# Four graph layers on one core: layer 1's output computed feature by feature, sums in a matmul of their own, two nodes per partition, and a new table of times

## The chip, the core and the metric

The kernel runs on one core of a Trainium2 chip. A core has five engines that each take their own instructions in order: TensorE (PE) multiplies matrices, VectorE (DVE), ScalarE (ACT) and GpSimd (POOL) work element by element, and SyncE (SP) starts the DMA transfers. The engines wait for each other through semaphores. The metric is the device time of one execution in microseconds (us); lower is better.

## What is computed

There are 64 graphs of 256 nodes with 512 features each. Every graph goes through four layers, and each layer adds its result to `x`. All numbers are 32-bit floats. Cut to what matters here:

```python
h = relu(layernorm(x))                                  # at the head of every layer
# layer 0
q, k = split(h @ Wqk.T); v = h @ Wv.T
x += softmax_over_nodes(sum_m((q @ k.T) * adj) / 8) * v
# layer 1: 8 heads of 64 features
feats = h @ W                                           # per head
dense = leaky_relu(e_self[i] + e_neigh[j], 0.2) - 1e10 * (1 - adj)
x += relu(softmax_over_j(dense) @ feats + b)            # heads side by side
# layer 2: 8 heads of 64 features
Xp = h @ Wp + bp; attn = tanh(adj * ((Xp @ C.T) @ Xp.T))
x += relu(attn @ Xp)
# layer 3
q, k = split(h @ Wqk); v = h @ Wv
x += softmax_over_nodes(sum(q * (adj @ k))) * v
```

The graphs do not depend on each other.

## The kernel before

One graph is cut into 140 named steps. `graph(b)` defines them, and each step issues a few instructions. Up to five graphs are in work at once, each in another layer. The order in which the steps are issued is written by hand: `TIMES` gives each step of a graph a time, `PERIOD` is the distance from one graph to the next, `FIRST` and `LAST` hold own times for the graphs at both ends, and `WEIGHTS` those for loading the weights. `Plan.run` sorts all steps by these times and chains the instructions of each engine in this order. The times are thus only an order: at run time an instruction starts when the one before it on its engine has been issued and its semaphores are there. If one of them waits, all behind it on the same engine wait.

Tiles come from fixed pools (`keep`): 8 PSUM banks (`bank`), 5 `xt` (a graph's `x`), 2 `hn`, 3 `ht`, 4 `pair`, and so on. `take` hands out the one that has been free longest, `done` gives it back.

What the change touches:

- **Node layout.** `load` (L629 to L634) puts node c*128+p on partition p. `adj` is loaded the same way. A second copy of it is loaded in 32-wide pieces (`blocks`), and `at` (L639) transposes it on DVE in 32x32 blocks.
- **Transposed activations.** Each layer's `st` (statistics, DVE), `rs`, `pw` (a power on POOL, L668), `sh`, `hn` (normalise, ACT, L680) make the normalised rows. `sq` (L613) transposes them in 32x32 blocks on DVE, `sw` (L700) writes the result to DRAM, and `ht` (L618, four DMAs in `gathered`) reads it back with the features on the partitions. Layer 2 does the same with `xp` (`sqx`, `swx`, `xpt`).
- **Matmul rows.** `rows` (L607) multiplies a chunk of 128 nodes of `ht`, as the stationary operand, by a weight of 128 to 512 columns, summed over four blocks of features.
- **Layer 1.** `fa`, `fb` compute the features and, in 16 more columns, the two score terms of each head; `fae`, `fbe` copy them out. A tile of `feats` has 65 columns per head: 64 features and a column of ones, set once (L464). `sendp` (L824, two transposes on PE), `senda` (L829, ACT) and `er` (L835) turn the score terms into rows in DRAM, and `enes` (L839, L840) reads these back to all partitions. `max0` to `max3` (L852) find the largest term of each row on DVE, `mxv` completes it, `mxp` (L873), `mxa` (L878) and `mr` (L884) turn it into rows, and `mb` (L888) reads them back to all partitions. For each pair p of heads, `ea` (L897, ACT) adds and applies the leaky relu, `eg` (L904, POOL) adds the mask `negt`, `eb` (L910, DVE) subtracts the maximum, `ex` (L916, ACT) takes the exponential.
- **Layer 1's output.** `po` (L928) multiplies with the exponentials as the stationary operand (128 nodes i) and 65 columns of `feats` as the moving one; the 65th column yields the sum of the weights. `pn` (L941, L945, DVE) divides by it and clips at zero, `pa` (L953, POOL) adds to `xt`.
- **Masks.** `neg` (L644), `negt` (L648) and `am` (L1094) run on POOL.
- **Layer 2's output.** `py` (L1030) already computes the other way round: 64 features of `xp` are stationary, 256 nodes move, and two heads fill the two halves of the partitions. `ye` (ACT, L1039) copies out with a relu; `sqy` (L1064), `swy` (L700) and `yr` (L1076) transpose through DRAM; `yg` (POOL, L1083) and `yv` (DVE) add to `xt`.

The matmul at the centre of the change is this:

```python
nc.tensor.matmul(po[:, h % 4, :], e[:, s, j, i * P:(i + 1) * P], feats[:, j, h, :],
                 start=(j == 0), stop=(j == NC - 1))
```

Of the kernel before, what the change touches and what calls it, by code (L numbers as in the profile page):

```python
# [9 lines left out]
F32 = mybir.dt.float32  # L10
# [13 lines left out]
UE = U + 1  # L24
# [12 lines left out]
PERIOD = 60.2  # L37
TIMES = {
    "load": 0.000, "at": 1.247, "st0": 5.280, "rs0": 5.300, "negt": 7.670, "pw0": 13.367, "sh0": 13.387,
    "hn0": 13.407, "sq0": 13.427, "sw0": 16.594, "ht0": 18.551, "qk1": 23.168, "qk0": 24.945, "qe0": 24.965,  # L40
    "qe1": 24.985, "pv01": 25.815, "score0": 27.291, "s0v": 27.311, "softp0": 29.436, "pv00": 31.771,
    "softv0": 32.366, "softa0": 33.344, "softw0": 35.861, "add0": 35.881, "st1": 39.861, "rs1": 39.881,
    "pw1": 40.011, "sh1": 40.031, "hn1": 40.638, "sq1": 43.586, "sw1": 46.132, "ht1": 57.350, "fa0": 57.370,
    "fa1": 57.371, "fb0": 57.372, "fae0": 57.934, "fae1": 58.840, "sendp": 58.860, "senda": 58.880, "er": 60.959,
    "neg": 61.845, "fb1": 64.147, "fbe0": 67.381, "enes": 67.749, "fbe1": 71.535, "max2": 74.244, "ea1": 75.256,
    "max0": 75.757, "max3": 76.069, "ea3": 77.200, "ea0": 78.017, "max1": 78.219, "mxv": 78.317, "mxp": 79.925,
    "ea2": 80.651, "eg2": 82.397, "mxa": 85.102, "eg0": 86.489, "mr": 87.558, "eg1": 88.075, "mb": 88.185,
    "eb0": 90.739, "eb2": 93.202, "ex0": 94.320, "eb1": 95.449, "eg3": 96.405, "po0": 97.573, "ex1": 97.708,
    "ex2": 99.827, "po2": 100.283, "eb3": 101.293, "ex3": 101.313, "po1": 102.298, "pn0": 106.351, "pa0": 108.061,
    "po3": 110.560, "pn1": 110.580, "pa1": 114.029, "st2": 114.049, "rs2": 114.069, "pw2": 114.089, "sh2": 117.872,  # L50
    "hn2": 117.892, "sq2": 120.365, "sw2": 126.933, "ht2": 134.926, "xp0": 134.946, "xp1": 140.660, "xe0": 141.890,
    "xe1": 147.360, "sqx": 147.380, "swx": 148.833, "xpt": 152.315, "xc": 161.371, "xcv": 174.104, "xca": 174.124,
    "ps0": 174.125, "tv1": 174.144, "ta1": 174.164, "tv0": 174.656, "ta0": 177.182, "ps1": 177.255, "tv2": 177.275,
    "ta2": 178.752, "tv3": 180.071, "ta3": 180.091, "am": 180.092, "py0": 181.534, "py1": 184.516, "ye0": 188.391,
    "ye1": 188.411, "sqy": 190.648, "swy": 192.764, "yr": 197.444, "yv": 199.505, "yg": 201.580, "st3": 202.086,
    "rs3": 203.471, "pw3": 205.848, "sh3": 205.868, "hn3": 207.396, "sq3": 207.856, "agg0": 209.112,
    "sw3": 211.920, "ga0": 215.679, "agg1": 217.655, "ht3": 218.179, "ga1": 220.247, "z0": 234.444, "z1": 245.189,
    "zv0": 245.866, "pv30": 248.297, "pv31": 251.239, "zv1": 261.554, "softp3": 263.233, "softv3": 264.096,
    "softa3": 267.934, "softw3": 282.911, "add3": 285.241, "store": 294.897,
# [3 lines left out]
    "wn0": 292.900, "mt0": 293.000, "wqk": 293.100, "mv0": 294.200, "wa": 294.700, "mm0": 295.100, "wv0": 295.500,  # L63
    "w11": 295.600, "w10": 296.200, "sa1": 296.700, "sa0": 297.000, "wn1": 298.500, "w13": 298.600, "mt1": 299.000,
    "b1": 299.400, "mv1": 299.500, "mm1": 299.800, "w12": 300.000, "sa3": 300.100, "sa2": 300.500, "w21": 300.700,
    "mk": 301.500, "c2": 301.800, "wn2": 303.200, "w20": 304.200, "mt2": 304.500, "mv2": 304.800, "mm2": 305.200,
    "wn3": 305.800, "mt3": 308.600, "w22": 309.100, "mv3": 309.500, "mm3": 309.600, "mkp": 310.600, "ma": 310.800,
    "w23": 311.300, "mkv": 313.400, "b2": 314.200, "room": 318.700, "wv3": 321.500,
# [3 lines left out]
        "load": 292.800, "st0": 293.300, "rs0": 293.400, "pw0": 293.500, "sh0": 293.600, "hn0": 293.700,  # L72
        "sq0": 293.800, "at": 294.000, "negt": 294.400, "sw0": 294.600, "ht0": 294.800, "qk0": 295.200,
        "qe0": 295.300, "qk1": 295.800, "qe1": 295.900, "score0": 296.000, "pv01": 296.100, "s0v": 296.400,
        "softp0": 296.500, "pv00": 296.800, "softv0": 296.900, "softa0": 297.100, "softw0": 297.200,
        "add0": 297.300, "st1": 297.400, "rs1": 298.000, "pw1": 298.100, "sh1": 298.300, "hn1": 298.700,
        "sq1": 298.800, "sw1": 299.600, "ht1": 300.300, "fa0": 300.900, "fae0": 301.300, "fa1": 301.600,
        "fae1": 301.700, "sendp": 302.200, "fb0": 302.300, "senda": 302.400, "er": 302.500, "enes": 303.300,
        "fbe0": 303.400, "ea3": 304.600, "ea2": 305.300, "neg": 305.500, "max1": 305.600, "ea1": 305.700,
        "max3": 305.900, "max0": 306.000, "max2": 306.100, "ea0": 306.500, "mxv": 306.600, "eg1": 306.800,  # L80
        "mxp": 307.100, "eg2": 307.200, "mxa": 307.500, "fb1": 307.700, "mr": 307.800, "eg3": 308.100,
        "mb": 308.400, "fbe1": 308.900, "eg0": 309.200, "eb1": 309.700, "eb2": 309.900, "eb0": 310.100,
        "eb3": 310.200, "ex2": 310.300, "ex0": 310.400, "ex3": 310.500, "ex1": 311.000, "po0": 311.100,
        "po2": 311.800, "po3": 312.100, "pn1": 312.800, "pa1": 313.000, "po1": 313.200, "pn0": 313.700,
        "pa0": 313.900, "st2": 315.100, "rs2": 315.700, "pw2": 315.800, "sh2": 316.000, "hn2": 316.400,
        "sq2": 317.100, "sw2": 318.500, "ht2": 320.700, "xp0": 322.900, "xe0": 323.000, "xp1": 323.100,
        "xe1": 324.200, "sqx": 324.300, "swx": 325.300, "xpt": 325.400, "xc": 327.200, "xcv": 327.300,
        "xca": 327.800, "ps0": 328.100, "tv1": 328.500, "tv0": 328.700, "ps1": 328.800, "ta1": 329.100,
        "tv2": 329.700, "ta0": 329.800, "py0": 329.900, "tv3": 330.400, "ta2": 330.600, "ta3": 330.800,
        "py1": 331.100, "ye0": 331.300, "ye1": 332.000, "sqy": 332.100, "am": 332.200, "swy": 333.400,  # L90
        "yr": 333.900, "yg": 334.700, "yv": 334.800, "st3": 335.000, "rs3": 335.600, "pw3": 335.700,
        "sh3": 336.100, "hn3": 336.200, "agg0": 336.500, "agg1": 336.800, "sq3": 337.200, "sw3": 337.500,
        "ht3": 338.900, "ga0": 339.400, "ga1": 339.700, "z0": 340.400, "zv0": 340.500, "z1": 340.900,
        "pv30": 341.200, "zv1": 341.400, "softp3": 341.800, "softv3": 342.000, "softa3": 342.100, "pv31": 342.200,
        "softw3": 342.400, "add3": 343.000, "store": 344.300,
    },
    {
        "load": 233.000, "st0": 233.700, "rs0": 233.900, "pw0": 234.100, "at": 234.300, "sh0": 234.700,
        "hn0": 234.800, "sq0": 235.200, "sw0": 235.500, "negt": 236.100, "ht0": 236.400, "qk0": 237.300,
        "qe0": 237.400, "qk1": 237.500, "qe1": 237.600, "score0": 237.700, "pv00": 238.700, "s0v": 239.100,  # L100
        "pv01": 239.500, "softp0": 240.600, "neg": 240.800, "softv0": 240.900, "softa0": 241.000,
        "softw0": 241.700, "add0": 241.800, "st1": 241.900, "rs1": 242.400, "pw1": 242.500, "sh1": 242.600,
        "hn1": 243.600, "sq1": 243.800, "sw1": 243.900, "ht1": 244.700, "fa0": 246.000, "fa1": 246.700,
        "fae0": 246.800, "fae1": 247.100, "sendp": 247.700, "senda": 248.000, "er": 248.100, "fb0": 248.600,
        "enes": 248.800, "fbe0": 249.100, "max2": 251.200, "ea3": 251.300, "max0": 251.400, "max1": 251.500,
        "max3": 251.700, "mxv": 252.300, "mxp": 252.400, "ea1": 252.500, "fb1": 253.100, "eg1": 253.300,
        "mxa": 253.600, "ea0": 254.200, "mr": 254.300, "ea2": 254.400, "eg2": 255.300, "mb": 256.400,
        "eg3": 256.500, "fbe1": 256.600, "eg0": 257.000, "eb2": 257.500, "eb0": 258.200, "eb3": 258.800,
        "ex2": 259.100, "eb1": 259.300, "ex3": 259.400, "po2": 259.500, "po3": 259.600, "ex0": 259.700,
# [308 lines left out]
def tile_four_gnn_layers(ctx: ExitStack, tc: tile.TileContext, x, adj, nodemask,  # L418
                         wqk0, wv0, w1, b1, a_self, a_neigh, w2, b2, c2t, wqk3, wv3, out):

    nc = tc.nc
    B = x.shape[0]

# [7 lines left out]
    rows_d = ctx.enter_context(tc.tile_pool(name="rows_d", bufs=12, space=DRAM))  # L434
    banks = ctx.enter_context(tc.tile_pool(name="banks", bufs=1, space=PSUM))

    plan = Plan(tc)

    def keep(kind, count, shape, pool=None):

# [728 lines left out]
```

## Time and profile before

| | |
|---|---|
| Median of three runs | 3894.62 us (3894.17 to 3900.92) |
| The profiled execution | 3905.45 us, of which its span 3903.3 us |
| Share of the span in which an engine is busy | PE 98%, DVE 78%, ACT 44%, POOL 32% |
| Mean busy share of the 16 DMA engines | 74.7% for the queue of SP |
| Packets under 512 bytes | 1493936 of 1657607 |

The span runs from the first to the last instruction in the profile. "Busy" counts the time in which an engine has an instruction under way; matmuls overlap, and their ends are modelled. A matmul of 32-bit floats appears as two instructions: `po` has 32 matmuls per graph, and the profile counts 4096 of them in 64 graphs. A line of the instruction groups gives source line, engine, operation, output and input, number, then the busy time in us and the mean duration of one in ns.

### The profile page before, as it was taken

Reading aid. Unit: us, or ns where it says so; the run is one execution under the profiler, and the core shown is the slowest. Engines: PE = TensorE matmul, PEld = TensorE weight load, DVE = VectorE, ACT = ScalarE, POOL = GpSimd, SP = SyncE. Lnnn points to the kernel's source line nnn. Section 1 sums busy time; section 2 is a strip of 40 time slices with the busy share of each in tenths; the row PEclk is TensorE's granted clock in tenths of the full one; section 3 lists DMA queues with packets and bytes.
Section 4 is the critical chain, followed back from the end, with each engine's and each line's share of the span. In section 5 each row is a group of like instructions: output and inputs, shape, how many; then the busy total and the mean of one; then the engine's idle time right before and its main releaser. Section 6 shows DMA issues by size and latency. Waiting matters only on the chain.

```text
span 3903.3 us, 53632 instructions
## 1 busy us (share of the span) xinstructions
PE 3811.1 (98%) x17474; PEld 2375.3 (61%) x17474; DVE 3033.7 (78%) x7641; ACT 1704.9 (44%) x3333; POOL 1264.8 (32%) x1098
## 2 busy tenths in 40 slices
PE   7999999999999999999999999999999999999989
PEld 4756566566566666666666666666566665665564
DVE  6887778777877877877777788788788778777774
ACT  2444444444444444444444444444444444444342
POOL 1332323323323323323323333333233233233231
PEclk9999999999999999999999999999999999999989
DMA  8666777777777788777777877777778777777754
GB/s 211 174 189 172 179 194 174 196 193 179 194 189 184 194 185 189 192 185 181 190 186 186 196 182 187 191 181 191 191 176 200 187 181 192 187 179 193 172 145 107
DMA packets 1657607, 717.62 MB, mean 184 GB/s; under 512 B 1493936, under 2 KB 1549296, under 8 KB 1632752
## 3 DMA queue, kind: packets, MB, share of 16 engines
q1 hardware_dynamic: 1657328, 714.19, 74.7%
q8 instruction: 140, 2.29, 0.3%
q14 instruction: 139, 1.14, 0.1%
HBM read 477.56 MB, written 236.45 MB: 183 GB/s over the span
## 4 chain that ended last, share of the span: by engine, by line
PE 74%; DVE 7%; DMA 4%; SPq 2%; issue 1%; POOL 1%; ACT 1%; DVEq 0%; POOLq 0%; ACTq 0%
PE bank L607 44%; PE bank L928 10%; PE bank L1016 6%; PE bank L1030 5%; PE bank L1102 5%; PE bank L994 3%; DVE junk L852 2%; DVE sq L613 1%; DMA hn<-sq_d 1%; SPq L618 1%; DMA ht<-sq_d 1%; DVE shift L673 1%; PE bank L768 1%; PE bank L718 1%; DVE stats L657 1%
## 5 line engine op out<-in xcount | busy, mean ns | idle before, releaser
L607 PE MATMUL bank<-w_s,ht 128*128 128x256 f32 (+2 forms) x3072 | 963.4, 464 | 30.6 <-DMA ht<-sq_d 24.5
L607 PE MATMUL bank<-wv_s,ht 128*128 128x512 f32 x2048 | 914.4, 594 | 0.1
L607 PEld LDWEIGHTS bank<-w_s,ht 128*128 128x128 f32 x3072 | 572.9, 192 | 364.4 <-issue 215.6
L607 PEld LDWEIGHTS bank<-wv_s,ht 128*128 128x128 f32 x2048 | 380.8, 191 | 426.2 <-issue 410.8
L904 POOL TENSOR_TENSOR pair<-pair,negt 128x1024 f32<-128x1024 f32 x256 | 600.5, 2367 | 50.6 <-ACT pair L897 46.4
L680 ACT ACTIVATE hn<-xt,shift,rstd 128x512 f32<-128x512 f32 x512 | 388.7, 806 | 448.6 <-DVE shift L673 430.3
L928 PEld LDWEIGHTS bank<-feats,pair 128*128 128x128 f32 x4096 | 485.0, 194 | 47.9 <-issue 25.5
L897 ACT ACTIVATE pair<-all,ec 128x256 f32<-128x256 f32 x1024 | 417.2, 494 | 200.1 <-DMA all<-er_d 196.3
L928 PE MATMUL bank<-feats,pair 128*128 128x65 f32 x4096 | 480.8, 276 | 10.2 <-ACT pair L916 10.2
L1055 ACT ACTIVATE pair<-pair 128x512 f32<-128x512 f32 x512 | 294.8, 623 | 420.6 <-DVE pair L1048 420.2
L852 DVE CUSTOM_DVE_ANT_0 junk<-all,adj 128x256 f32<-128x256 f32 x1024 | 444.0, 434 | 35.2 <-DMA all<-er_d 2.1
L607 PE MATMUL bank<-m_s,ht 128*128 128x512 f32 x1024 | 465.9, 599 | 1.3 <-DVE pair L1048 0.8
L668 POOL TENSOR_TENSOR rstd<-rstd,power 128x2 f32<-128x2 f32 x256 | 180.6, 706 | 813.4 <-DVE rstd L664 804.9
L1048 DVE TENSOR_TENSOR pair<-bank,at 128x512 f32<-128x512 f32 x512 | 327.4, 683 | 107.7 <-PE bank L1016 107.0
L1083 POOL TENSOR_TENSOR xt<-xt,hn 128x512 f32<-128x512 f32 x64 | 111.5, 1742 | 924.6 <-DMA hn<-sq_d 657.9
L613 DVE STREAM_TRANSPOSE sq<-hn 128x512 f32<-128x512 f32 x512 | 337.7, 690 | 58.9 <-ACT hn L680 58.9
L657 DVE BATCH_NORM_STATS2 stats<-xt 128x6 f32<-128x512 f32 x512 | 327.2, 680 | 36.4 <-POOL xt L1083 28.6
L910 DVE TENSOR_TENSOR pair<-pair,all 128x1024 f32<-128x1024 f32 x256 | 325.9, 1292 | 9.9 <-DMA all<-m_d 7.5
L607 PEld LDWEIGHTS bank<-m_s,ht 128*128 128x128 f32 x1024 | 189.2, 190 | 213.5 <-issue 207.1
L953 POOL TENSOR_TENSOR xt<-xt,o 128x256 f32<-128x256 f32 x256 | 181.2, 729 | 386.6 <-DVE rs L941 225.1
L916 ACT ACTIVATE pair<-pair 128x1024 f32<-128x1024 f32 x256 | 262.2, 1047 | 45.1 <-DVE pair L910 39.6
L1016 PE MATMUL bank<-xc,xpt 64*128 64x256 f32 x2048 | 255.8, 389 | 1.8 <-ACT xc L1002 1.0
(77 smaller groups left out, 3866.9 us busy)
## 6 DMA issues: line engine op xcount, KB each, us to landing
sq_d<-sq SPq DMA_DIRECT2D x384, 512.0 KB
ht<-sq_d SPq DMA_DIRECT2D x1024, 128.0 KB
all<-er_d SPq DMA_DIRECT2D x128, 1024.0 KB
all<-m_d SPq DMA_DIRECT2D x64, 1024.0 KB
xt<-in_x_dram SPq DMA_DIRECT2D x64, 512.0 KB
xpt<-sq_d SPq DMA_DIRECT2D x256, 128.0 KB
hn<-sq_d SPq DMA_DIRECT2D x256, 128.0 KB
out_dram<-xt SPq DMA_DIRECT2D x64, 512.0 KB
```

Source lines behind the costliest of these rows:

```text
L607: nc.tensor.matmul(p, ht[:, k, c * P:(c + 1) * P], w[:, k], start=(k == 0), stop=(k == KC - 1))
L613: nc.vector.transpose(sq.rearrange("p (r k c i) -> p c k r i", r=4, k=KC, c=NC)[:, c], t[:, c])
L657: nc.vector.bn_stats(stats[:, c, :], g["xt"][:, c, :])
L680: nc.scalar.activation(hn[:, c, :], g["xt"][:, c, :], AF.Relu, bias=st["shift"][:, c:c + 1], scale=st["rstd"][:, c:c + 1])
L852: nc.vector.tensor_tensor_reduce(junk, g["en"][:, h, :], g["adj"][:, c, :], 1.0, -BIG, OP.add, OP.max, st["mx"][:, c, h:h + 1])
L897: nc.scalar.activation(e[:, s, j, :], g["es"][:, h, :], AF.Prelu, bias=st["ec"][:, j, H + h:H + h + 1], alpha=0.2)
L904: nc.gpsimd.tensor_tensor(e, e, g["negt"][:, None].to_broadcast([P, 2, NC, N]), OP.add)
L910: nc.vector.tensor_tensor(e, e, g["m"][:, 2 * p:2 * p + 2, None, :].to_broadcast([P, 2, NC, N]), OP.subtract)
L928: nc.tensor.matmul(po[:, h % 4, :], e[:, s, j, i * P:(i + 1) * P], feats[:, j, h, :], start=(j == 0), stop=(j == NC - 1))
L1016: nc.tensor.matmul(ps[s][:, m, :], g["xpt"][half, p, m * P:(m + 1) * P], g["xc"][half, p, :], start=True, stop=True)
L1048: nc.vector.tensor_tensor(th[:, s], g[f"ps{p}{s}"].rearrange("p (m n) -> p m n", m=NC), g["at"], OP.mult)
L1055: nc.scalar.activation(g[f"th{p}"][:, s], g[f"th{p}"][:, s], AF.Tanh)
```

## The change

1. Node 2p+c is on partition p (before: node c*128+p). `load` and `store` move two nodes per partition in one piece. `chunk(t, c)` picks every second column, and every matmul that took 128 neighbouring columns of `ht`, `at` or `xpt` takes these. The DVE transposes write or read with a step of two, and `gathered` and `blocks` now move pieces of 64 numbers (before: 32).
2. `po` has the features as the stationary operand (64 columns) and 256 nodes of the exponentials as the moving one, two heads in the two halves of the partitions. The column of ones is gone.
3. The sums are computed apart: `eh` adds the two halves of the exponentials on POOL, `su` multiplies them by a 32-column tile with one column of ones, once per head, into the four quarters of a bank. `se` (ACT), `sp` (two transposes on PE) and `sr` (DVE) bring the reciprocals to the nodes' partitions.
4. `oe` (ACT) copies the output with a relu; `sqo`, `swo`, `or` bring it back to the nodes' partitions through DRAM, and `oa0`, `oa1` (POOL) multiply by the reciprocals and add to `xt`. `back` serves layers 1 and 2. `pn` and `pa` are gone.
5. `sendp` and `senda` become `send`, `mxp` and `mxa` become `mxt`: each is a transpose in 32x32 blocks on DVE. `er` and `mr` write in four DMAs each.
6. `neg`, `negt` and `am` move from POOL to ACT.
7. `TIMES`, `WEIGHTS`, `FIRST` and `LAST` are new throughout, and `PERIOD` is 59.0 (before: 60.2). There are now 150 steps.

```diff
-PERIOD = 60.2
+PERIOD = 59.0
...
-    small = ctx.enter_context(tc.tile_pool(name="small", bufs=6))
+    small = ctx.enter_context(tc.tile_pool(name="small", bufs=5))
...
+    def chunk(t, c):
+        return t.rearrange("p (n c) -> p c n", c=NC)[:, c]
...
-    keep("feats", 2, [P, NC, H, UE])
+    keep("feats", 2, [P, NC, D])
...
-    keep("o", 1, [P, NC, 4 * U])
+    keep("mx", 1, [P, NC, S])
+    keep("half", 2, [P, 2, N])
...
+    ones = consts.tile([P, 2, S], F32)
+    nc.gpsimd.memset(ones, 0.0)
+    for q in range(2):
+        nc.gpsimd.memset(ones[:, q, q:q + 1], 1.0)
...
-            nc.tensor.matmul(p, ht[:, k, c * P:(c + 1) * P], w[:, k], start=(k == 0), stop=(k == KC - 1))
+            nc.tensor.matmul(p, chunk(ht[:, k], c), w[:, k], start=(k == 0), stop=(k == KC - 1))
...
-            nc.vector.transpose(sq.rearrange("p (r k c i) -> p c k r i", r=4, k=KC, c=NC)[:, c], t[:, c])
+            nc.vector.transpose(sq.rearrange("p (r k i c) -> p c k r i", r=4, k=KC, c=NC)[:, c], t[:, c])
...
-            nc.sync.dma_start(t.rearrange("p k (c b i) -> b p (k c) i", c=NC, b=4)[i],
-                              sq_d.rearrange("(b d) (r f i) -> b (d r) f i", b=4, r=4, i=S)[i])
+            nc.sync.dma_start(t.rearrange("p k (b e) -> b p k e", b=4)[i],
+                              sq_d.rearrange("(b d) (r k e) -> b (d r) k e", b=4, r=4, k=KC)[i])
...
-            nc.sync.dma_start(g.take("xt"), x[b].rearrange("(c p) d -> p c d", p=P))
+            nc.sync.dma_start(g.take("xt"), x[b].rearrange("(p c) d -> p c d", c=NC))
...
-            nc.gpsimd.tensor_scalar(g.take("negt", HP), g["at"], -1.0, -NEG_BIG, op0=OP.add, op1=OP.mult)
+            nc.scalar.activation(g.take("negt", HP), g["at"], AF.Identity, scale=-NEG_BIG, bias=far)
...
+        def back(name, cols):
+            @step(f"sq{name}")
+            def _():
+                nc.vector.transpose(g.take("sq").rearrange("p (b k c i) -> p k b c i", b=4, k=HP, c=NC),
+                                    g[cols].rearrange("p k (b i c) -> p k b c i", b=4, c=NC))
+                g.done(cols)
+            @step(f"sw{name}")
+            def _():
+                out_by_squares()
+            @step(f"{name}r")
+            def _():
+                y = g.take("hn", NC, name="y" if name == "y" else "yo")
+                y = y.rearrange("p c d -> p (c d)").rearrange("p (a f) -> p a f", a=4)
+                for q in range(4):
+                    nc.sync.dma_start(y[q * S:(q + 1) * S], st["sq_d"].rearrange("(a i) (q f) -> q i a f", a=4, q=4)[q])
...
-        @step("sendp")
-        def _():
-            pn = g.take("bank", name="pn")
-            for c in range(NC):
-                nc.tensor.transpose(pn[:E, c * P:(c + 1) * P], st["ec"][:, c, :], ident)
...
+        @step("send")
+        def _():
+            st["er"] = er = work.tile([P, N // 4], F32, name="er", bufs=1)
+            nc.vector.transpose(er.rearrange("p (i c) -> p c i", c=NC), st["ec"])
...
-            nc.sync.dma_start(st["er_d"], st["er"])
+            for i in range(4):
+                nc.sync.dma_start(st["er_d"][:, i * 2 * S:(i + 1) * 2 * S], st["er"][i * S:i * S + E])
...
+                for j in range(NC):
                     for s in range(2):
                         h = 2 * p + s
-                        for j in range(NC):
-                            nc.tensor.matmul(po[:, h % 4, :], e[:, s, j, i * P:(i + 1) * P], feats[:, j, h, :],
-                                             start=(j == 0), stop=(j == NC - 1))
+                        nc.tensor.matmul(po[s * U:(s + 1) * U, p % 2, :], feats[:, j, h * U:(h + 1) * U],
+                                         e[:, s, j, :], start=(j == 0), stop=(j == NC - 1))
...
+            @step(f"eh{p}")
+            def _():
+                e = g[f"e{p}"]
+                nc.gpsimd.tensor_tensor(g.take("half", name=f"h{p}"), e[:, :, 0, :], e[:, :, 1, :], OP.add)
+                g.done(f"e{p}")
...
+            @step(f"su{q}")
+            def _():
+                if not q:
+                    g.take("bank", name="su")
+                for r in range(2):
+                    for s in range(2):
+                        t = 2 * r + s
+                        nc.tensor.matmul(g["su"][t * S:(t + 1) * S, :N], ones[:, q], g[f"h{2 * q + r}"][:, s, :],
+                                         start=(q == 0), stop=(q == 1))
...
+            @step(f"oe{q}")
+            def _():
+                if not q:
+                    g.take("cols", name="oc")
+                nc.scalar.activation(g["oc"][:, 2 * q:2 * q + 2, :], g[f"po{q}"].rearrange("p (r n) -> p r n", r=2),
+                                     AF.Relu)
...
+        def divide(c):
+            @step(f"oa{c}")
+            def _():
+                y = g["yo"].rearrange("p c d -> p (c d)").rearrange("p (a k c i) -> p c k a i", a=4, k=HP, c=NC)[:, c]
+                rs = st["rs"][:, c].rearrange("p q t -> p (q t)").rearrange("p (k s) -> p s k", s=2)
+                for s in range(2):
+                    half = y[:, :, 2 * s:2 * s + 2]
+                    nc.gpsimd.tensor_tensor(half, half, rs[:, s, :, None, None].to_broadcast([P, HP, 2, S]), OP.mult)
+                xt = g["xt"][:, c, :].rearrange("p (k a i) -> p k a i", k=HP, a=4)
+                nc.gpsimd.tensor_tensor(xt, xt, y, OP.add)
+                g.done("yo")
...
-                nc.gpsimd.tensor_scalar(g["at"][:, m, :], g["at"][:, m, :], mask_c[:, m, b:b + 1], None, op0=OP.mult)
+                nc.scalar.activation(g["at"][:, m, :], g["at"][:, m, :], AF.Copy, scale=mask_c[:, m, b:b + 1])
```

The order in which `TIMES` puts PE's steps in the new plan, written within one period (the number is how many periods after its graph's loading the step runs): fb1 (2), xc (3), po0, po1 (2), ps0 (3), po2, su0, po3 (2), ps1 (3), su1 (2), fa1, fa0 (1), sp (2), z0, z1 (4), py0, py1 (3), softp3, pv31, pv30 (4), qk0, qk1 (0), fb0 (1), score0 (0), xp0 (2), softp0 (0), xp1 (2), pv00, pv01 (0), agg1, agg0 (3).

## The prediction

> **What bounds the kernel now.** I read the page's busy times first, then the chain that ended last, then that chain in order of time, and last PE's timeline.
>
> ```profile
> span 3903.3 us, 53632 instructions
> PE 3811.1 (98%) x17474; PEld 2375.3 (61%) x17474; DVE 3033.7 (78%) x7641; ACT 1704.9 (44%) x3333; POOL 1264.8 (32%) x1098
> PE 74%; DVE 7%; DMA 4%; SPq 2%; issue 1%; POOL 1%; ACT 1%; DVEq 0%; POOLq 0%; ACTq 0%
> ```
>
> PE is busy for 98% of the span. That alone does not show a PE at its limit, because the ends of matmuls are modelled; but 74% of the chain that ended last is PE too. The same chain, with start and length of each piece:
>
> ```profile
> 559.33 5.59 PE bank L607 x24
> 564.92 0.22 PE bank L824 x2
> 565.14 3.60 PE bank L1030 x32
> 568.74 15.66 PE bank L607 x40
> 584.40 0.22 PE bank L873 x2
> ...
> 588.05 0.22 PE bank L718 x2
> ...
> 601.47 3.52 PE bank L928 x32
> 604.99 1.78 PE bank L994 x8
> 606.77 3.52 PE bank L928 x32
> 610.29 1.93 PE bank L1016 x16
> ...
> 617.78 5.59 PE bank L607 x24
> ...
> 2566.15 5.59 PE bank L607 x24
> ```
>
> The block of 24 (fa0, fa1, fb0) comes once per graph. From 559.33 to 617.78 are 58.45 us, filled by PE pieces without a gap: this is PE's work for one graph. From 559.33 to 2566.15 lie 34 graphs, 59.02 us each, so stalls cost 0.57 us per graph. 64 x 59.02 = 3777; the other 126 us of the span are the ends. Only what shortens PE's 58.45 us, or adds a stall to it, counts.
>
> **What the Trainium skill says.** "TensorEngine Tiling (Array Packing)", Tiling Modes: a stationary operand of 64 columns leaves room for two tiles, one of 32 for four, working at once. The trace agrees for 64: L1030 moves 256 columns in 3.60/32 = 113 ns, a full-width L607 of 256 columns takes 1.83/8 = 229 ns. No row shows 32. "TensorE: Matmul & The Clock Gate", Measured speedup vs the span model, has 2.38 for three column tiles. "SBUF — State Buffer", Door 1, states lines of 16 bytes, full rate with two reads per line; a step of two floats keeps two. The trace shows no such weight load; DVE's transposes of `hn` read every fourth float and take 690 ns for 512, about one per cycle. "GPSIMD Engine Reference", 3.1: about 2.6 cycles per element with two inputs; L904 takes 2367 ns for 1024, which fits.
>
> **PE, part by part, per graph.**
> - `po`: out go two L928 pieces of 3.52 us, 7.04. In come 16 matmuls, 32 instructions, of L1030's form: 3.60.
> - Transposes: out go L824 and L873, 0.44. In come `sp`'s two, as L718: 0.22.
> - `su`: 8 matmuls, 16 instructions of 256 columns. At 229 ns alone 3.66; four at once 0.92; in pairs 1.81. I take 1.2, since the skill's three tiles gain 2.38, so four about 3.
> - `chunk` changes the step of the weight loads and not their number: zero, discussed below.
>
> Sum: -7.04 + 3.60 - 0.44 + 0.22 + 1.2 = -2.46. PE's work falls from 58.45 to 56.0 us.
>
> **The other engines** must fit 56 us. DVE now 3033.7/64 = 47.4: minus `pn` (108.7+45.0)/64 = 2.4, plus `sqo` as L1064 1.24, `sr` as two L941 0.35, two small transposes about 0.45 (estimate from 512 in 690 ns and a fixed part): 47.0. POOL 19.8: minus `pa`, `am`, `neg`, `negt` (181.2+118.1+40.0+40.4)/64 = 5.9; plus four `eh` of 512 elements, between L953 (729 ns for 256) and L904, 1.28 each, 5.1; plus `oa`, per c two products (0.73 to 0.96 each) and an addition as L1083 (1.74), 6.4 to 7.3 in all: about 26. ACT 26.6: plus `neg`, `negt` as L680 1.6, `am` as L897 1.0, `oe` 1.2, `se` 0.36, minus two copies 0.72: 30. None reaches 56. SP gains six row writes (0.34 each), `swo` 0.33, `or` 4 x 0.44: 4.1 us of some 35 used. The DMA engines get fewer packets: about 25,900 per graph now, of which `ht` and `xpt` are 5 x 512 KB / 128 B = 20,480; that number halves, `blocks` halves, the new round trip adds about 640: some 15,000. I book no gain.
>
> **The added wait.** Layer 1's output now leaves PE, goes through DRAM and POOL, and only then can layer 2 normalise. From po3's end to xp0 the parts are `oe1` 0.60 (L1039), `sqo` 1.24, write and read back, `oa` 6.9, statistics to the last `ht` issue, landing. The read back is taken from layer 2's present one:
>
> ```profile
> 2053.75 0.66 SPq L700 DMA_DIRECT2D sq_d<-sq  x1
> 2054.51 2.26 SPq L1076 DMA_DIRECT2D hn<-sq_d  x4
> ```
>
> ```profile
> 2060.47 0.69 DVE L1083 TENSOR_TENSOR xt<-xt,hn 128x512 f32<-128x512 f32 x1 [3.11 <-DMA hn<-sq_d]
> ```
>
> That is 2060.47 - 2053.75 = 6.72. Statistics starting at 2019.15 had their `ht` issued by 2030.86:
>
> ```profile
> 2019.15 1.28 DVE L657 BATCH_NORM_STATS2 stats<-xt 128x6 f32<-128x512 f32 x2
> ```
>
> ```profile
> 2027.42 3.44 SPq L618 DMA_DIRECT2D ht<-sq_d  x4
> ```
>
> 11.71; and `ht` issued by 2002.04 let PE start at 2004.50, 2.46. Together 0.60+1.24+6.72+6.9+11.71+2.46 = 29.6. In the new order PE has between po3 and xp0: ps1 1.93, su1 0.6, fa1 and fa0 3.76, sp 0.22, z 6.9, py 3.60, softp3 0.22, pv 6.88, qk 1.78, fb0 1.83, score0 0.84: 28.6. So xp0 waits about 1.0 us per graph. Behind oa on POOL stands pw2 of the same chain; behind ht2 on SP stands yr, so layer 2's output of another graph, and DVE's yv, slip with it. If POOL or DVE hold each other up (sh, 0.16 us, once took 2.29 beside eg), the chain grows; with half the packets it shrinks. Bounds: 0 to 3 us.
>
> Two smaller waits are new. su1 needs the last `eh`: two of these after ex3 take 2.6 us on POOL, while PE has po3 and ps1, 2.8; I book nothing, up to 0.7 if `eh` costs as much as L1083. On ACT, `negt` waits for `at` and `am` for the last `tv`; both are done by DVE well before in the new order, and ACT is idle for half of the period, so what stands behind them (`ea`, `qe`) is not held: nothing.
>
> The other long returns have room. From pv01 to fa1 the chain is the last addition (0.7), statistics to `ht` (11.7), landing 2.5: 14.9, against agg 3.5, fb1 1.83, xc 1.78, four po 3.6, ps 3.86, su 1.2: 15.8. The stall of 0.57 that exists now is partly this kind; I keep none beside the 1.0, as xp0's wait gives the rest time, and put the error in the range.
>
> **Sum.** 56.0 + 1.0 = 57.0 per graph; 64 x 57.0 + 126 = 3774 for the span, 3776 for the execution, against its own 3905.45. That is -3.3%; the median shown, 3894.62, is 0.28% below the profiled run, so about 3765.
>
> **Rivals.**
> 1. The return is longer, 31 to 32 us, for instance because `or` lands late behind other transfers or POOL's products cost more: xp0 waits 2.5 us, 58.5 per graph, 3870 for the span, 3860 as a median. For it: POOL already waited 657.9 us in all for such a landing (`xt` L1083 on `hn<-sq_d`). Against: the packets halve. From 31.6 us on (28.6 + 3.0, which is 59.0 per graph) the kernel is not faster.
> 2. Slower: strided weight loads cost more. Place: the matmuls whose load is as long as their stream, qk (16 instructions, 1.78/16 = 111 ns each), score0 (8), ps (32), 56 per graph. At double length 56 x 0.11 = 6.2 us: 57.0 + 6.2 = 63.2, 4171 for the span, about 4160. It decides from 2.0/56 = 36 ns more per load. Against: the lines of 16 bytes, and DVE's full rate at a wider step. For: PE reads nothing this way now.
> 3. The sums do not run side by side: su costs 3.66, 2.46 more, PE's work 58.5; with the longer filling at xp0 (from su1) the wait falls to nothing: about 58.6 per graph, 3870. If the wait stays, 59.5 and slower, 3930.
>
> That the table itself is the cost, its order making waits that I haven't found, would look like rival 1.
>
> **How the numbers follow.** Forecast 57.0 per graph: 0.58, own range 55.9 to 58.0, 3695 to 3830. Rival 1: 0.25, of which 0.04 same and 0.06 slower. Rival 2: 0.11, nearly all slower, 0.01 faster. Rival 3: 0.06, of which 0.02 slower. Faster (by over 0.2%, about what a measurement of this kernel can tell from no change): 0.58 + 0.15 + 0.01 + 0.04 = 0.78; same 0.04; slower 0.06 + 0.10 + 0.02 = 0.18. The range from 3670 to 3940 leaves out rival 2 and the worst of rivals 1 and 3.
>
> **What would show it.** In PE's timeline: L928's successor in pieces of 32 instructions in 3.6 us; su's 16 in about 1.2; loads of ht still near 190 ns and qk's 16 in 1.8. PE's idle time before xp0, released by DMA `ht`, about 1 us per graph. The block of fa comes every 57 us. Wrong it would be if PE's pieces of L607 grow (rival 2), if su's piece is 3.6 (rival 3), or if PE stands idle for 2 us or more per graph, before xp0 or elsewhere (rival 1).

## The result: no change, and the profile after

The changed kernel took 3894.13 us (median of four runs, 3892.97 to 3897.74); the kernel before, beside it, 3894.39 us. The ratio is 0.9999 with a 95% interval of 0.9982 to 1.0016. The forecast was 3765. All times are medians of the executions in the fast state; this matters only for the single graph in experiment 5, where it makes the difference 11.9 us in place of the 10.9 that an earlier expectation gives.

The page after answers to the one before with these lines (the engines' busy time, then the engines' shares of the chain that ended last):

```profile
span 3892.8 us, 52870 instructions
...
PE 3677.6 (94%) x16322; PEld 2126.0 (55%) x16322; DVE 3060.4 (79%) x7449; ACT 1872.2 (48%) x3653; POOL 1531.4 (39%) x1229
...
PE 46%; DVE 20%; DMA 17%; SPq 8%; issue 5%; POOL 3%; ACT 2%; DVEq 0%; ACTq 0%; POOLq 0%
```

PE does 133.5 us less (3811.1 before), 2.1 us per graph. But the span is only 10.5 us shorter, and PE's share of the chain falls from 74% to 46%: it now waits for others. Here is that chain for part of a graph in the middle, with start and length of each piece:

```profile
2029.04 1.72 DVE shift L706
...
2042.19 3.91 PE bank L639 x16
...
2057.17 6.89 PE bank L639 x16
2064.06 0.02 issue
2064.08 0.53 SPq L650
...
2066.00 2.81 DMA ht<-sq_d
2068.81 0.25 issue
2069.06 3.68 PE bank L639 x8
```

There are two ways into PE here for which the forecast booked nothing. The block of `fa` at 2042.19 hangs on layer 1's `ht`, and that on a `shift` (the step `sh`) which holds the chain for 1.7 us at 2029.04; half of all `shift` take 0.16 or less. And xp0 at 2069.06 hangs on an `ht` whose transfer starts when the matmuls ending at 2064.06 (layer 3's `pv`) give a buffer back. In this example its data had landed only 0.1 us before. In the stretch from 600 to 3600 us SyncE, with the data of an `ht` landed, still waited for such a buffer 55 times, 29.5 us in all and 1.1 at most:

```profile
SPq L650 <- PE bank L639: 29.5, 55, 1.1
```

PE's longest waits in the same stretch, by what ended them (total, times, longest), after and then before:

```profile
PE bank L639 <- DMA ht<-sq_d: 51.5, 65, 1.5
PE bank L966 <- ACT pair L954: 26.1, 46, 1.0
```

```profile
PE bank L607 <- DMA ht<-sq_d: 11.5, 12, 1.7
```

The two after are 78 of PE's 91 us of idle time in that stretch; before it was 21 us in all. Counted over 48 graphs in the middle, PE now idles 1.76 us per graph: 1.00 between the end of pv01 and `fa` (for `ex` before `po`, and for `ht` before `fa`) and 0.76 before xp0.

To split the time, I took the distance from one graph to the next on PE's timeline (`agg` of graph 9 to `agg` of graph 59, divided by 50), and what 64 such distances leave of the span, "the ends". The ratios are to executions of the kernel before that were taken beside each run:

| run | median us | ratio to the kernel before, 95% | us per graph | PE idle, 600 to 3600 us | ends us |
|---|---|---|---|---|---|
| before | 3894.39 | | 59.03 | 21 | 125 |
| after | 3894.13 | 0.9999 (0.9982 to 1.0016) | 58.12 | 91 | 173 |
| a_nolock | 3838.32 | 0.9851 (0.9834 to 0.9868) | 57.23 | 57 | 175 |
| a_ht4 | 3870.30 | 0.9929 (0.9914 to 0.9944) | 57.84 | 82 | 163 |
| a_ht4_nolock | 3817.74 | 0.9802 (0.9786 to 0.9818) | 56.82 | 49 | 178 |
| a_noprod | 3884.08 | 0.9969 (0.9953 to 0.9984) | 58.11 | 92 | 158 |
| a_all_noprod3 | 3792.86 | 0.9744 (0.9727 to 0.9761) | 56.48 | 35 | 172 |
| b_nolock | 3876.37 | 0.9947 (0.9932 to 0.9962) | 58.74 | 15 | 114 |
| b_ht4_nolock3 | 3880.01 | 0.9965 (0.9950 to 0.9979) | 58.81 | 17 | 115 |
| b_layout | 3896.76 | 1.0003 (0.9996 to 1.0009) | 59.03 | 4 | 117 |

The names are those of the experiments below; a_ are edits of the changed kernel, b_ of the kernel before. So the forecast's span of 3774 us was missed by 119: 64 x (58.12 - 57.0) = 72 us in the steady part and 173 - 126 = 47 us at the ends.

This division is rough. The last of the 50 distances already belongs to the end of the run (49.9 us after, 56.0 before). Without it the time per graph is 58.28 us after and 59.09 before, the ends are 163 and 121 us, and the miss divides into 82 and 37. The kernel before was also profiled in an execution 11 us above its median, which makes 0.17 us per graph. What is left of the gain is about 0.64 us per graph, not 0.91. Differences between the a_ rows change by 0.03 us at most.

### The profile page after: what moved, and what is told of

It reads as the page before. It is cut to its first block, busy times and chain, and to the rows that moved or that the text cites. A ratio compares the mean times of both kernels' runs of the same rounds, so it can differ in the third digit from the quotient of the medians.

```text
span 3892.8 us, 52870 instructions
## 1 busy us (share of the span) xinstructions
PE 3677.6 (94%) x16322; PEld 2126.0 (55%) x16322; DVE 3060.4 (79%) x7449; ACT 1872.2 (48%) x3653; POOL 1531.4 (39%) x1229
## 2 busy tenths in 40 slices
DMA packets 967435, 784.71 MB, mean 202 GB/s; under 512 B 788913, under 2 KB 859121, under 8 KB 942577
## 4 chain that ended last, share of the span: by engine, by line
PE 46%; DVE 20%; DMA 17%; SPq 8%; issue 5%; POOL 3%; ACT 2%; DVEq 0%; ACTq 0%; POOLq 0%
PE bank L639 34%; DVE sq L645 7%; DMA ht<-sq_d 6%; SPq L650 5%; DMA sq_d<-sq 5%; PE bank L1111 4%; PE bank L966 3%; DVE pair L948 2%; DVE junk L896 2%; DMA hn<-sq_d 2%; PE bank L1097 2%; DVE stats L690 2%; DMA blocks<-in_adj_dram 2%; DVE xt L775 2%; DVE shift L706 1%
## 5 line engine op out<-in xcount | busy, mean ns | idle before, releaser
L639 PEld LDWEIGHTS bank<-w_s,ht 128*128 128x128 f32 x3072 | 587.4, 198 | 381.3 <-issue 288.2
L942 POOL TENSOR_TENSOR pair<-pair,negt 128x1024 f32<-128x1024 f32 x256 | 604.5, 2374 | 117.2 <-ACT pair L935 117.2
L639 PEld LDWEIGHTS bank<-wv_s,ht 128*128 128x128 f32 x2048 | 397.3, 197 | 444.8 <-issue 442.8
L975 POOL TENSOR_TENSOR half<-pair 128x512 f32<-128x512 f32 x256 | 331.3, 1306 | 593.1 <-PE bank L989 328.0
L896 DVE CUSTOM_DVE_ANT_0 junk<-all,adj 128x256 f32<-128x256 f32 x1024 | 472.8, 462 | 31.4 <-issue 0.2
L639 PE MATMUL bank<-m_s,ht 128*128 128x512 f32 x1024 | 455.5, 597 | 8.2 <-DMA ht<-sq_d 6.8
L935 ACT ACTIVATE pair<-all,ec 128x256 f32<-128x256 f32 x1024 | 433.4, 497 | 9.8 <-DMA all<-er_d 9.8
L966 PE MATMUL bank<-pair,feats 128*64 128x256 f32 x2048 | 272.4, 401 | 62.2 <-ACT pair L954 62.0
L954 ACT ACTIVATE pair<-pair 128x1024 f32<-128x1024 f32 x256 | 264.0, 1050 | 118.4 <-DVE pair L948 111.2
L948 DVE TENSOR_TENSOR pair<-pair,all 128x1024 f32<-128x1024 f32 x256 | 303.4, 1223 | 15.3 <-DMA all<-m_d 14.4
L1032 POOL TENSOR_TENSOR hn<-hn,rs 128x256 f32<-128x256 f32 x256 | 152.3, 617 | 392.4 <-DMA hn<-sq_d 317.7
L761 ACT ACTIVATE bank<-bank,nmax 128x256 f32<-128x256 f32 x128 | 56.8, 443 | 504.5 <-DVE nmax L756 504.5
```

The source lines that it names most:

```text
L639: nc.tensor.matmul(p, chunk(ht[:, k], c), w[:, k], start=(k == 0), stop=(k == KC - 1))
L896: nc.vector.tensor_tensor_reduce(junk, g["en"][:, h, :], g["adj"][:, c, :], 1.0, -BIG, OP.add, OP.max, g["mx"][:, c, h:h + 1])
L935: nc.scalar.activation(e[:, s, j, :], g["es"][:, h, :], AF.Prelu, bias=st["ec"][:, j, H + h:H + h + 1], alpha=0.2)
L942: nc.gpsimd.tensor_tensor(e, e, g["negt"][:, None].to_broadcast([P, 2, NC, N]), OP.add)
L948: nc.vector.tensor_tensor(e, e, g["m"][:, 2 * p:2 * p + 2, None, :].to_broadcast([P, 2, NC, N]), OP.subtract)
L966: nc.tensor.matmul(po[s * U:(s + 1) * U, p % 2, :], feats[:, j, h * U:(h + 1) * U], e[:, s, j, :], start=(j == 0), stop=(j == NC - 1))
```

## Experiment 1: VectorE held up by GpSimd

The timeline of the kernel after shows both engines at the two long small instructions (start, length, engine, line, operation; in brackets the idle time before it and what ended it):

```profile
2018.25 4.69 POOL L942 TENSOR_TENSOR pair<-pair,negt 128x1024 f32<-128x1024 f32 x2
...
2021.61 1.36 DVE L769 TENSOR_SCALAR w<-w,tot 128x2 f32<-128x2 f32 x1
...
2028.97 2.35 POOL L942 TENSOR_TENSOR pair<-pair,negt 128x1024 f32<-128x1024 f32 x1
2029.04 2.30 DVE L706 SCALAR_TENSOR_TENSOR shift<-mv,rstd 128x2 f32<-128x2 f32 x1 [0.49 <-POOL rstd L701]
```

L706 writes two numbers per partition and lasts until POOL's `eg` (L942) is done; L769 too ends with it. The mean of L769 is 825 ns, with a median of 229; before it was 264. L706 has a mean of 648 ns with a median of 160, hardly different from before (665). The Trainium skill, "SBUF — State Buffer", Who interferes with whom, names such a cause: VectorE and GpSimd share a pair of ports, and an instruction of VectorE that reads two tensors in SBUF, or runs in a mode with two ports, waits for the whole of a GpSimd instruction already under way. One with a single tensor input and outside these modes does not. That can be tried without moving anything: the same products, one column at a time, with the second factor as a scalar operand.

```diff
-                nc.vector.scalar_tensor_tensor(st["shift"], st["mv"][:, :, 0], -1.0, st["rstd"],
-                                               op0=OP.mult, op1=OP.mult)
+                for c in range(NC):
+                    nc.vector.tensor_scalar(st["shift"][:, c:c + 1], st["mv"][:, c, 0:1], st["rstd"][:, c:c + 1], -1.0,
+                                            op0=OP.mult, op1=OP.mult)
...
-                nc.vector.tensor_scalar(st["w"], st["w"], st["tot"], None, op0=OP.mult)
+                for c in range(NC):
+                    nc.vector.tensor_scalar(st["w"][:, c:c + 1], st["w"][:, c:c + 1], st["tot"], None, op0=OP.mult)
```

In the changed kernel (a_nolock):

> The changed kernel with sh and softw as two one-column instructions each, which read one tensor and scalars and should not have to wait for POOL's additions. Lock theory: w (825 ns on average) and shift (648 ns) fall to about 0.2 us each, 1.5 to 2.5 us less between xp1 and po2 per graph; 3790 to 3840 us. Return theory: the same loop passes through this stretch, so it predicts a gain too, as large as the stretch gets shorter, down to PE's 56.0 us per graph. Buffer theory: 3880 to 3895. If the one-column forms wait for POOL as well, nothing changes.

In the kernel before (b_nolock):

> The same edit of sh and softw in the kernel before. It is held by PE in the middle (58.45 of 59.03 us per graph), so all theories give at most 0.5 us per graph: 3860 to 3895 us.

Measured: 3838.32 us, 1.5% less, and 3876.37 us, 0.5% less. In the timeline of a_nolock the same pair now looks like this (the two columns of `shift` count as x2):

```profile
2051.32 2.37 POOL L944 TENSOR_TENSOR pair<-pair,negt 128x1024 f32<-128x1024 f32 x1
2051.38 0.34 DVE L707 TENSOR_SCALAR shift<-mv,rstd 128x1 f32<-128x1 f32 x2 [0.49 <-POOL rstd L701]
```

The two instructions take 0.34 us beside an `eg` that runs on for 2 us, and over the whole run the 512 of `shift` take 206 ns each on average. What the page says of both kinds holds here, with one addition: L769 had a single tensor input already and was held. By the page it must then have run in a mode with two ports, which no view shows; what changed for it is one column in place of two. PE's waits for `ex` (L954 before, 26.1 us) are gone from the stretch between 600 and 3600 us, and its idle time there falls from 91 to 57 us: between pv01 and `fa` from 1.00 to 0.27 us per graph, before xp0 from 0.76 to 0.68. Part of the hold only moves: `eb`, which reads two tensors in SBUF, takes 1502 ns on average in place of 1223, with nearly the same median (1218 and 1210). `shift` and `w` were not tried apart. The kernel before gains only a third as much. Its idle time in the stretch falls from 21 to 15 us, and where the rest of its gain of some 20 us lies was not followed.

## Experiment 2: a fourth ht buffer

a_ht4 gives `ht` a fourth buffer, in the space of the second `xpt`.

```diff
-            keep("xpt", 2, [P, HP, N], late)
+            keep("xpt", 1, [P, HP, N], late)
+            plan.pools["ht"].append(late.tile([P, KC, N], F32, name="ht3"))
```

> The changed kernel with a fourth ht buffer (it takes the place of the second xpt, which is never needed at the same time). Buffer theory: ht2's read back waits for pv30, which frees the oldest ht, and so xp0 starts late; with a fourth buffer the 0.6 to 1.1 us per graph go, 3825 to 3855 us. Return theory (the DRAM and POOL return of layer 1's output sets xp0): the write of the squares lands only just before pv30 ends, so within 0.4% of 3894. Lock theory (VectorE held by POOL between xp1 and po2): no change either.

It took 3870.3 us, 0.7% less than the kernel before: 0.27 us less per graph than the changed kernel, or 17 us in 64, and some 10 at the ends. This lies in none of the three ranges: the buffer theory expected 0.6 to 1.1 us per graph. SyncE's waits for a buffer fell by more than half (6 of the 28 left are for the one `xpt`):

```profile
SPq L651 <- PE bank L640: 12.4, 28, 0.6
```

PE's idle time between pv01 and `fa` stays at 1.02 us per graph, and its wait before xp0 falls from 0.76 to 0.48. The late buffer costs something, but it is the smaller part. Both edits together (a_ht4_nolock):

> The changed kernel with both edits that helped by themselves: the fourth ht buffer (in place of the second xpt buffer) and the one-column forms of sh and of softw's product. Alone they took 0.7% and 1.5% off. Theory (two separate causes, each a stall of PE of its own): what is left in the run with the one-column forms is PE waiting for ht, 46.4 us in 59 waits between 600 and 3600 us, most of them for a buffer; the fourth buffer takes most of that and some 10 us of the ends: 3785 to 3810 us, a period of about 56.6 us per graph against PE's work of 56.0 to 56.1. Rival (one cause seen twice: the hold by POOL and the late buffer delay the same waits, and removing either already gives what there is): 3825 to 3840 us.

3817.74 us, 2.0% less, where the single gains add up to 2.2%: nearly separate causes. The time lies above the theory's 3785 to 3810 and below the rival's 3825 to 3840. The steady part is now 56.82 us per graph, the forecast's 57.0. The chain in the middle of this run has hardly a stall:

```profile
2009.42 10.49 PE bank L640 x40
2019.90 0.88 PE bank L824 x8
2020.78 0.10 issue
2020.88 3.68 PE bank L640 x8
```

The piece of 40 is `pv`, `qk` and fb0; score0 and xp0 follow, with 0.1 us of waiting. The periods without any stall take from 56.1 us on here (the one shown 56.3), which is PE's work for a graph. This kernel is faster than both of the others.

The same two edits in the kernel before:

> The kernel before with the same two edits: one-column forms of sh and softw's product, and a fourth ht buffer in place of the second xpt buffer. It sets a bound on what the change is worth when both kernels have them. Theory (the kernel before is at PE's work and has little left to gain): 58.5 us per graph, 3855 to 3877 us, at most 0.5% under what the one-column forms alone gave; the changed kernel with both, 3818 us, is then 1 to 1.5% faster. Rival (the edits help either kernel alike): about 3820 us, and the change is worth nothing.

3880.01 us, no better than the one-column forms alone and 3 us above the theory's range. With these waits gone from both kernels, the change is worth 0.9802/0.9965 = 0.984; beside the kernel before with one-column forms alone it is 0.9802/0.9947 = 0.985. That is about 1.5%.

## Experiment 3: the return through DRAM and POOL

Does the longer way of layer 1's output hold PE? a_noprod leaves out the four products of `oa`, that is the division by the sums. That shortens the way from po3 to xp0 by the 2.4 us that the products take.

```diff
-                for s in range(2):
-                    half = y[:, :, 2 * s:2 * s + 2]
-                    nc.gpsimd.tensor_tensor(half, half, rs[:, s, :, None, None].to_broadcast([P, HP, 2, S]), OP.mult)
```

> The changed kernel without the two products in each oa (the division by the sums is left out; all else is issued), 2.4 us less on POOL per graph. Return theory: the path from po3 to xp0 takes 29.3 us and becomes 26.9, and the whole loop xp0 to xp0 falls below PE's 56.0 us; 56.3 to 57.0 per graph instead of 58.1, 3780 to 3830 us. Lock theory or buffer theory alone: the loop is held elsewhere, 3870 to 3895 us.

3884.08 us, only 0.3% less, and none of it in the steady part: 58.11 us per graph against 58.12. The gain lies at the ends (158 for 173). The theory that the return holds PE was wrong as I had put it. With the two other causes gone, the same edit (a_all_noprod3) was expected to tell more:

> The changed kernel with the fourth ht buffer and the one-column forms, and without the four products of POOL in oa (the division of layer 1's output by its sums is left out). It asks what the return through DRAM and POOL costs once the two other causes are gone. If it still holds PE in the middle, 2.4 us less on that way give up to 0.7 us per graph, 3770 to 3790 us. If it only costs at the ends, where the products alone gave 14.7 us before: 3800 to 3810 us. If it costs nothing: 3815 to 3820 us.

3792.86 us, 25 us less than a_ht4_nolock: 64 x (56.82 - 56.48) = 22 us of it in the steady part. The time lies just above the 3770 to 3790 expected if the return still holds PE. So the return looks like one of several ways into PE of nearly the same length: shortening it alone gave its place to the next, and once the others are shorter it counts. One rival stands: the edit also takes 2.4 us of GpSimd work per graph away, beside which VectorE may have been held, and the two were not tried apart. This version leaves out the division; it only shows what a shorter way would be worth.

## Experiment 4: the node layout alone

b_layout is the kernel before with point 1 of the change and nothing else. Besides `chunk` at every matmul that takes 128 nodes, its core is:

```diff
-            nc.sync.dma_start(t.rearrange("p k (c b i) -> b p (k c) i", c=NC, b=4)[i],
-                              sq_d.rearrange("(b d) (r f i) -> b (d r) f i", b=4, r=4, i=S)[i])
+            nc.sync.dma_start(t.rearrange("p k (b e) -> b p k e", b=4)[i],
+                              sq_d.rearrange("(b d) (r k e) -> b (d r) k e", b=4, r=4, k=KC)[i])
```

> The kernel before with the node layout alone: node 2p+c on partition p, transfers of ht, xpt, blocks and at in pieces of 256 bytes in place of 128, and every stationary operand that is cut by nodes read at a step of two floats. Theory (strided weight loads are free, and the transfers were not what PE waited for): PE's work stays at 58.45 us per graph, the period within 58.5 to 59.0, 3855 to 3895 us, with the DMA engines' share down from 75% to about 60%. Rival (the halved packets are where the changed kernel's gain came from): under 3850 us. Rival (the strided loads cost and something else in the change hid it): over 3910 us.

3896.76 us: no change, within 0.1%, and 2 us above the theory's range. The DMA engines' share fell from 74.7% to 59.7%, and PE's idle time in the middle from 21 to 4 us, but the time per graph stayed. PE's own work grew, which the theory had excluded. Its chain shows this:

```profile
1001.27 3.71 PE bank L932 x32
...
1046.95 5.33 PE bank L610 x24
1052.27 0.88 PE bank L772 x8
```

These are a half of `po`, a piece with `qk` in it, and score0; they took 3.52, 5.22 and 0.84 us before (L928, L607, L768). With two pieces of `po` that is 2 x 0.19 + 0.11 + 0.04 = 0.53 us per graph: a matmul whose stationary operand is read at a step of two floats takes 6 ns more (0.19/32) where the load is about as long as the stream, and a period without a stall takes 59.0 us for 58.45. In the changed kernel `po` has other stationary operands, so of these 0.53 us only the last two terms, 0.15, apply to it. If the transfers gave something, the loads took it. Whether fewer packets or PE's longer work removed the stalls, this run does not tell, as either would.

## Experiment 5: the ends

The first 32, the first 14 and the first graph only, in both kernels; and the way of layer 1 shortened for 14 graphs. Each is one number in the last line (and a_noprod_14 the edit of experiment 3 besides):

```diff
-    plan.run(weights, graph, B)
+    plan.run(weights, graph, B // 2)
```

> The changed kernel on the first 32 graphs only; the other half of the output isn't computed. With b_half it divides the time into a part per graph and a part that does not depend on their number. If the changed kernel's loss sits at the ends (173 us against 125 us, read from the traces of the full runs), it should take 173 + 32 x 58.12 = 2033 us here, and be slower than the kernel before by 15 to 22 us (48 - 32 x 0.92). If the two kernels simply cost the same per graph, the difference should be 0 (within 5 us).

> The kernel before on the first 32 graphs only; the other half of the output isn't computed. 125 + 32 x 59.03 = 2014 us, if the ends are what the full trace shows; the difference to a_half is what counts: 15 to 22 us if the loss sits at the ends, 0 if it does not.

> The changed kernel on the first graph only; the other 63 parts of the output aren't computed. With one graph no work of another hides anything, so the time is the weights' preparation and one graph's chain of steps. Theory (the ends are longer because one graph's own chain is: layer 1's output now takes the way through DRAM and POOL, about 0.6 + 1.2 + 6.7 + 5.1 = 13.6 us, where before it took two steps of VectorE and two of POOL, about 5): 8 to 20 us more than the kernel before on one graph. Rival (the chain is the same and the table's order of the first and last graphs makes the ends): within 5 us of it.

> The kernel before on the first graph only; the other 63 parts of the output aren't computed. The number to set beside the changed kernel's on one graph: 8 to 20 us less if the longer chain of one graph makes the ends, within 5 us if it does not.

> The changed kernel on the first 14 graphs only, which is little more than the eleven that have a table of times of their own (six first, five last); the other 50 parts of the output aren't computed. On one graph it took 10.9 us more than the kernel before, on 32 18.9 more, on 64 as long. If the loss at the ends arises in the filling and emptying of the pipeline as a whole (40 to 48 us, less what the steady part gains): 31 to 36 us more than the kernel before on 14 graphs. If the ends cost only what one graph's chain costs: 0 to 5 us more.

> The kernel before on the first 14 graphs only; the other 50 parts of the output aren't computed. The number to set beside the changed kernel's: 31 to 36 us less if the whole filling and emptying is longer, 0 to 5 us less if only one graph's chain is.

> The changed kernel on the first 14 graphs, without the four products of POOL in oa (the division of layer 1's output by its sums is left out, and 50 parts of the output). The way from po3 to xp0 is 2.4 us shorter by it. If the filling pays for the length of that way several times, one graph after the other: 10 to 15 us less than the changed kernel on 14 graphs, as in the full run. If it pays once: 2 to 3 us less.

| graphs | before us | after us | difference us |
|---|---|---|---|
| 1 | 188.40 | 200.31 | +11.9 |
| 14 | 950.42 | 973.98 | +23.6 |
| 32 | 2003.54 | 2022.43 | +18.9 |
| 64 | 3894.39 | 3894.13 | -0.3 |

The changed kernel starts with a loss and earns it back: from 32 to 64 graphs it gains 19.2 us, 0.6 per graph. The difference of the half runs came out as the ends theory had it (15 to 22), while each was some 10 us shorter than expected. The 14 graphs came out between the two expectations, 23.6 where 31 to 36 or 0 to 5 were expected; with the gain of 0.6 per graph added back, 32 us of loss are there by then, and 38 in the half runs, not the 48 read from the traces. The corrected division of the result, 163 - 121 = 42, is nearer.

The single graph shows where it begins. Chain of the kernel before (in an execution of 191.26 us, 2.9 above the table's), then of the changed one:

```profile
87.14 11.51 PE bank L928 x64
...
112.82 9.27 PE bank L607 x16
```

```profile
91.05 3.94 PE bank L966 x24
...
122.02 9.81 PE bank L639 x16
```

Before, `po` ends at 98.65 and xp0 starts at 112.82: 14.2 us. After, 94.99 to 122.02: 27.0 us. The way out of layer 1 is 12.9 us longer and its matmuls 7.6 us shorter on this chain (only the last 24 of `po`'s 32 are on it after); with 3.9 us that it is late already at `po`, xp0 comes 9.2 us later. a_noprod_14 took 962.11 us, 11.9 less than a_14, for a way that is 2.4 us shorter. This is as expected if the filling pays for the length of that way several times, here about five, one graph after the other. Which graphs pay is not shown, and the edit also takes work off GpSimd.

How much of the rest comes from the order in `FIRST` and `LAST` stays open; no other order was tried. The granted clock of TensorE was not separated either. In the first 300 us of the full runs it was 0.91 after and 0.96 before, in the last 300 it was 0.95 in both. In the single graph it was 0.62 during the 11.51 us of `po` shown above and 0.71 during the 3.94, so these pieces can't be compared as work.

## Why the prediction failed

- **PE's work, 58.45 to 56.0 us:** right. `po` takes 1.88 + 2 x 1.01 = 3.90 (forecast 3.60), `su` 2 x 0.57 = 1.14 (1.2), and a graph without a stall from 56.1 on. Rival 3 (sums not side by side) is refuted by `su`.
- **Strided weight loads cost nothing:** nearly. 0.53 us per graph in b_layout, 6 ns per load where rival 2 needed 36; it is refuted. One argument against it was misread: DVE's transposes of `hn` (690 ns) read runs of 32 neighbouring floats. Those that read every fourth float are of `xp`, and they take 1102 ns for the same size, so VectorE does not keep its rate at that step:

```profile
L613 DVE STREAM_TRANSPOSE sq<-hn 128x512 f32<-128x512 f32 x512 | 337.7, 690 | 58.9 <-ACT hn L680 58.9
L613 DVE STREAM_TRANSPOSE sq<-xp 128x512 f32<-128x512 f32 x128 | 136.0, 1102 | 0.0
```

- **DMA engines, 15,000 packets per graph, no gain booked:** right. 967435/64 = 15,116, and b_layout is worth nothing as a whole.
- **The return, 29.6 us from po3 to xp0:** right as a length (29.3 between 871.41 and 900.73, 30.1 on average of 48 graphs), and the wait before xp0, 0.76 us, is near the 1.0 booked. There is luck in both: 0.28 us of the wait went with the fourth `ht` buffer, which the forecast did not have in mind, and the parts of the length are off in both directions: the way to DRAM and back took 11.8 us for 8.6, `oa` 5.1 for 6.9, statistics to xp0 12.4 for 14.2.
- **The step that failed** is "The other long returns have room. From pv01 to fa1", with 14.9 us against 15.8 us of PE's work, and its end "I keep none beside the 1.0, as xp0's wait gives the rest time, and put the error in the range". From the end of pv01 to `fa` it is 16.9 us on average of 48 graphs, and PE idles 1.00 us of it. What was missing is VectorE held by GpSimd on this way. It was in view: "sh, 0.16 us, once took 2.29 beside eg" was written down as a thing that could make the chain grow, and no cost was put on it, although the mean of 665 ns against a median of 160 told already that it was no single case. New in the changed kernel is `w`, on the same way, with 825 ns on average in place of 264. With one-column forms the idle time on this way falls to 0.27 us, and 0.88 us of the time per graph go. The second missing wait, for one of the three `ht` buffers, was not looked for: 0.27 us per graph alone, 0.42 on top of the first edit. Together the two edits remove 1.30 us, and with 56.8 us per graph the forecast's 57.0 comes out.
- **The other failed term** is "the other 126 us of the span are the ends", carried over unchanged from the old kernel. It is 173 by the table and 163 as corrected, so 37 to 47 us were missed. The new way of layer 1's output was priced only where other graphs' work hides it; experiment 5 shows that it costs at the ends, but not how much of this loss is its own. a_ht4_nolock has the forecast's time per graph and misses its span of 3774 us by 40.
- **The rivals:** rival 1 had the right size (58.5 us per graph, 3860), but another cause: the return is hardly longer than forecast. What it called "order making waits that I haven't found" is nearer.

## What to carry to other kernels

When PE's work falls below a wait that used to be hidden, count all the ways into PE, buffers included, before pricing one of them: here several were of nearly the same length, and shortening the return alone gave nothing in the steady part. A small VectorE instruction with a mean far above its median may be held by something; if it stands on the path, find out by what, and try another form. Here one tensor input was not enough, and one column with a scalar operand was. And when a change trades engine time for a longer way through DRAM, price the way at both ends of the run too, where less work hides it; here the filling seems to have paid for it several times.

## What the runs showed of the hardware

- A VectorE instruction on two numbers per partition took up to 2.31 us beside a GpSimd tensor operation, and two one-column instructions for the same result 0.34 us. Of the 768 one-column instructions in a_nolock the longest took 0.24 us.
- Four tiles of 32 columns: 8 instructions of 256 columns in 0.57 us, 71 ns each, where a full-width one takes 229: 3.2 times as fast. The Trainium skill, "TensorEngine Tiling (Array Packing)", Theoretical Speedup, has up to 4 for 32 columns.
- A 32-bit stationary operand read at a step of two floats cost 6 ns per matmul of 110 ns in `po` (b_layout).
- VectorE's transposes of 512 numbers per partition took 690 ns reading neighbouring numbers and 1102 ns reading every fourth (the kernel before).
